# Denominators of eight heads at once in the last batch, filters loaded later, weight sums kept on chip, and two steps in halves: attention and convolution layers in fp32

## The chip, the cores and the metric

The kernel runs on one core of a Trainium2 chip. The metric is the device time of one execution in microseconds (us), taken as the median of several runs. All arithmetic is fp32. The engines are TensorE (PE in the profile, PEld its weight loads), VectorE (DVE), ScalarE (ACT), GpSimd (POOL) and SyncE (SP); SP and GpSimd also issue the transfers (DMAs) between HBM and on-chip memory.

## The reference

Four images of 1024 channels and 32 x 32 positions go through two layers. The first is attention over the 1024 positions, with 16 heads of 64; the second is a bottleneck of three convolutions with batch norms.

```python
# layer 0, x is (4, 1024 tokens, 1024 channels)
qkv = (x @ w_qkv.T + b_qkv).reshape(B, N, 3, nh, hd)
q, k, v = (qkv[:, :, 0], qkv[:, :, 1], qkv[:, :, 2])
q = _apply_rope(q, cos, sin); k = _apply_rope(k, cos, sin)
q = _rmsnorm(q.reshape(B, N, inner), q_norm_w).reshape(B, N, nh, hd)
k = _rmsnorm(k.reshape(B, N, inner), k_norm_w).reshape(B, N, nh, hd)
scores = jnp.einsum('bqhd,bkhd->bhqk', q, k) * scale
attn = jax.nn.softmax(scores, axis=-1)
ctx = jnp.einsum('bhqk,bkhd->bqhd', attn, v).reshape(B, N, inner)
out = _rmsnorm(ctx @ w_proj.T, norm_out_w) + residual
# layer 1
out = jax.nn.relu(_bn(_conv(x, w1, b1, 1, 0), g1, be1))       # 1x1, 1024 -> 256
out = jax.nn.relu(_bn(_conv(out, w2, b2, 1, 1), g2, be2))     # 3x3, 256 -> 256
out = _bn(_conv(out, w3, b3, 1, 0), g3, be3)                  # 1x1, 256 -> 1024
out = jax.nn.relu(x + jax.nn.softplus(residual_scale)[0] * out)
```

`_bn` takes its mean and variance over all four images.

## The kernel before, in words

**Products.** The four projections (q, k, v and the output y) are computed by Strassen's scheme: a 1024 x 1024 weight matrix and the tokens are split into 2 x 2 blocks, and seven products of sums of blocks replace eight. For q and k of batch 0, `project` does this once: 28 products of four 128 x 128 x 512 matmuls each. For each of the four groups it needs sums of four weight blocks, which `operands` makes on VectorE (L236 to L239) right before they are used: w_q_0b to w_q_3b, then w_k_0b to w_k_3b. All other projections (`project2`) use two levels: each of the seven outer products (`OUTER`: A11, A12, S2, S3, S1, S4, A22) is again split into seven. Of its seven weight tiles, three are quarters of the outer operand, and four are sums of its quarters. The outer sums (SUMS: S2, S1, S3, S4, called block sums here) are kept in the HBM buffer `wd`, the inner ones in `wd2`.

**Preparing the sums of v.** While q of batch 0 is projected, `prepare_blocks` loads four blocks at a time on GpSimd's queue, makes four block sums in place (L409 to L412) and stores them to `wd`. Then `prepare` (the parts k = 0 to 6 of `parts_of[WV]`) loads the four quarters of an outer operand (through `quarter`, L383), sums them (L392 to L395) and stores four results to `wd2` (L397). For parts 2 to 5 the quarters come back from `wd`. Where these tiles lie is given by `pieces_of`: before, the blocks and parts 0, 1, 6, 2 go through the 16 pieces of `unused`, and parts 3, 4, 5 and the first part of q's weights (for later batches) through `room`, the buffer in which v is put later (`rq` in the profile).

**Order.** On VectorE, ScalarE, TensorE and GpSimd the order is that in which the program emits its instructions (`manual_schedule`). A counter `pace["at"]` is raised by `product_done` after each product. `after(n, step)` emits a step n products later; `waiting` holds steps, such as the eight rope turns of q (`turn`, L701, with its GpSimd transfers at L705), that are emitted when there is room. `weight_parts(parts, first, step, lag, alloc)` loads part i at product first + i * step and makes its sums lag products later. An engine executes in order: a step that waits for its data holds up all that was emitted after it on that engine.

**Attention.** `attention` is called twice for each batch, for 512 queries each (c = 0, 1), and goes through eight pairs of heads (hp). For a pair, TensorE makes eight tiles of scores (L765), ScalarE takes their exponentials (L772), VectorE adds these up into the denominators (L776, L778), and TensorE multiplies them by v (L786). In the ordinary way, the denominators of two pairs are summed over the 128 partitions by four matmuls with `ones` (L817). In batches 1 and 2, with c = 0, `fold` is set instead: `halve` adds the upper half of the partitions to the lower by transfers on GpSimd's queue (L828 to L831), so that two pairs share one tile, and `sum_of_eight` makes the sums of eight heads with four matmuls by `halves` (L837), two pairs after they are complete. The tiles are those of the tags T0 and T2. Then the inverses are spread by transfers, and `mean_of_v` multiplies the outcome by them (L742) and adds the bias on GpSimd (L743).

`extra` is a list of VectorE steps spread over the 16 pairs of a batch. In batch 3 they are `filters()`: it first issues nine loads of the 3 x 3 filters on SP's queue (L1053), into the tags T0, T1, T2; then five steps (`sums_of`, L1060 to L1063, three on VectorE and one halving on ScalarE) make the transformed filters. `slow` holds GpSimd transfers that add the residual to an earlier batch's outcome (L1190).

**Convolutions.** The 3 x 3 one works on 2 x 2 output tiles: VectorE transforms a padded image first along rows (`across`, L1330, four results j = 0 to 3, named `cols`), then along columns (`down`, L1344, four rows, named `V`; both names are at L1325 in the profile). `uv` multiplies the outcome by the filters, those of j = 1, 2 before those of j = 0, 3. `first_channels` transforms the first half of the channels of image 0, while TensorE is still at the last products of the 1x1 convolution. `outputs` transforms back, and at the last image makes the batch norm and relu of all four images; ScalarE does images 0 and 2 whole (L1428), VectorE images 1 and 3 (L1430, L1431). The third convolution (L1526) reads them.

Of the kernel before, what the change touches and what calls it, by code (L numbers as in the profile page):

```python
# [13 lines left out]
ALU = mybir.AluOpType  # L14
# [71 lines left out]
def program(ctx, tc, x, wblk, w2, w3, vecs, cos, sin, out, bad):  # L86
# [71 lines left out]
    with tc.tile_pool(name=f"st{u}", bufs=2) as st, ExitStack() as s:  # L158
# [258 lines left out]

        def pieces(name):
            return [flat(chunk(f"w_{name}_{i}")) for i in range(4)]
# [325 lines left out]
        def attention(b, c, q_all, k_all, v, probs_, late, ready, extra, slow, steps_in_all, load_parts, fold):  # L745
# [4 lines left out]
            for hp in range(NHP):  # L750
# [58 lines left out]
                for _ in range(len(extra) - -(-steps_in_all * max(slots - 1 - c * NHP - hp, 0) // slots)):  # L809
                    extra.pop(0)()  # L810
# [235 lines left out]
        def filters():  # L1046

            steps = []
            raw = t_tiles("w2")
            taps = w2.rearrange("p (c k f) -> p c k f", c=NPT, k=9)  # L1050
            for dy in range(3):
                for dx, slot in enumerate((0, 1, 3)):
                    nc.sync.dma_start(  # L1053
                        raw[dy][:, slot, :].rearrange("p (c f) -> p c f", c=NPT), taps[:, :, 3 * dy + dx, :]
                    )
            two = [tp.tile([P, 2, CH], F32, tag=n, name=f"u2_{n}") for n in ("cos", "sin")]

            def sums_of(g0, g1, g2, new):

                nc.vector.tensor_tensor(new, g0, g2, ALU.add)  # L1060
                nc.scalar.mul(g1, g1, 0.5)
                nc.vector.scalar_tensor_tensor(g1, new, 0.5, g1, ALU.mult, ALU.add)
                nc.vector.tensor_tensor(new, new, g1, ALU.subtract)  # L1063

            for dy in range(3):
                r = raw[dy]
                steps.append(lambda r=r: sums_of(r[:, 0], r[:, 1], r[:, 3], r[:, 2]))
            for h in range(2):
                js = slice(2 * h, 2 * h + 2)
                steps.append(lambda h=h, js=js: sums_of(*(raw[dy][:, js] for dy in range(3)), two[h]))  # L1070
            for i in range(4):
                for j in range(4):
                    uw[i, j] = two[j // 2][:, j % 2] if i == 2 else raw[(0, 1, None, 2)[i]][:, j]
            return steps
# [61 lines left out]
        for b in range(B):  # L1136
# [8 lines left out]
            if b == 0:  # L1145
                unused = kp.tile([P, NT, N], F32, tag="k", name="unused")
                parts = blocks_of(WV) + [parts_of[WV][k] for k in (0, 1, 6, 2)]
                weight_parts(parts, 8, 2.4, 4, pieces_of(unused))
            elif b == 1:
                weight_parts([parts_of[WK][5]], 9, 0, 4, pieces_of(room[:, : NT // 2, :]))  # L1150
# [6 lines left out]
            if b == 0:  # L1157
                parts = [parts_of[WV][k] for k in (3, 4, 5)] + [parts_of[WQ][0]]
                weight_parts(parts, 2, 4.5, 4, pieces_of(room))
# [25 lines left out]
            if b == B - 1:  # L1185
                extra = filters()
# [11 lines left out]
            if b in (1, 2):  # L1198

                fold[0] = [tp.tile([P, NH, CH], F32, tag=t, name=f"den_{b}_{t}") for t in ("T0", "T2")]  # L1200
            for c in range(NCH):
                attention(
# [129 lines left out]
        def down(b, i, row, j=None):  # L1332
# [3 lines left out]
            if j is None:  # L1336
                d = cols.rearrange("p j (r q) c -> p q j r c", q=2)
                e = d[:, 0, :, :TR], d[:, 1, :, :TR], d[:, 0, :, 1:], d[:, 1, :, 1:]
                out = vt[b, i][:, row].rearrange("p j (r c) -> p j r c", r=TR)
# [12 lines left out]
        def first_channels():  # L1352
            norm1(0)
            fill(0, 0)
            for step in transform(0, 0):
                step()
# [47 lines left out]
        def outputs(b, f, h):  # L1404
# [18 lines left out]
            if b == B - 1:  # L1423
                n2 = norm_of(h2stats[:, f], col("g2", f), col("be2", f), f"2_{f}")
                for i in range(B):
                    z = h2[i, f]
                    if i % 2 == 0:
                        nc.scalar.activation(z, z, AF.Relu, bias=n2[1], scale=n2[0])  # L1428
                    else:
                        nc.vector.tensor_scalar(z, z, n2[0], n2[1], ALU.mult, ALU.add)  # L1430
                        nc.vector.tensor_scalar(z, z, 0.0, None, ALU.max)  # L1431
# [190 lines left out]
```

## Time and profile before

| what | us |
|---|---|
| median of three runs (2679.37 to 2683.2) | 2679.48 |
| the profiled execution | 2678.03 |
| its span, from first to last instruction | 2676.1 |

| engine | busy share of the span |
|---|---|
| TensorE, matmuls | 99% |
| TensorE, weight loads | 62% |
| VectorE | 79% |
| ScalarE | 42% |
| GpSimd | 17% |

A line of a timeline has the start, the busy time, the engine, the line of the code, the operation, what it writes and reads, and how many instructions are merged; in square brackets the idle time ahead of it and what ended it. A line of the waits has the engine and the work that waited, what it waited for, the total, the number of waits and the longest. A line of the windows has the stretch and its length, the busy time of TensorE, its weight loads, VectorE, ScalarE and GpSimd, then the granted clock of TensorE (1.00 is full), the busy share of the DMA engines, and GB/s.

### The profile page before, as it was taken

The page shows a single profiled execution, that of the slowest core. Times are in us where ns is not written, and L with a number is a line of the kernel's source. Part 1 is how long each engine was busy: PE and PEld are TensorE (multiplying, and loading weights), DVE is VectorE, ACT ScalarE, POOL GpSimd, SP SyncE. Part 2 cuts the span into 40 slices and gives each one's busy share as a digit, 9 for nine tenths or more (in the row PEclk, how much of TensorE's full clock was granted, in tenths as well). Part 3 has the DMA queues.
Part 4 walks back from the last instruction along what each step waited for, and adds up shares of the span by engine and source line. Part 5 has one row for each costly group of instructions (what it writes and reads, how often), then busy time and mean ns, then how long its engine had stood idle before and what let it go on. Part 6 is the DMA issues. An engine that isn't in the chain of part 4 may idle for free. (4 is left out here: it accounts for less than half of the span.)

```text
span 2676.1 us, 32605 instructions
## 1 busy us (share of the span) xinstructions
PE 2646.2 (99%) x11354; PEld 1652.0 (62%) x11354; DVE 2108.7 (79%) x2528; ACT 1111.9 (42%) x1547; POOL 464.7 (17%) x568
## 2 busy tenths in 40 slices
PE   9999999999999999999999999999999999999997
PEld 4448533488888333688886333888884335846843
DVE  5577899998787866888879667887978678877987
ACT  2222455523442655433343555233525654312266
POOL 2551233301001221200111222100111211010000
PEclk9999999999999999999999999999999999999999
DMA  7897766667567451446675541665783313583165
GB/s 277 315 288 205 209 230 220 231 210 242 174 183 217 80 104 44 157 151 224 190 197 146 92 77 32 214 207 173 193 233 87 69 40 114 172 281 100 63 237 204
DMA packets 258252, 460.28 MB, mean 172 GB/s; under 512 B 35552, under 2 KB 130576, under 8 KB 258080
## 3 DMA queue, kind: packets, MB, share of 16 engines
q1 hardware_dynamic: 213552, 309.09, 35.6%
q0 software_dynamic: 44528, 149.02, 21.8%
q8 instruction: 93, 1.52, 0.2%
q14 instruction: 79, 0.65, 0.1%
HBM read 331.62 MB, written 97.01 MB: 160 GB/s over the span
## 5 line engine op out<-in xcount | busy, mean ns | idle before, releaser
L772 ACT ACTIVATE p<-sc 128x1024 f32<-128x1024 f32 x512 | 476.2, 1045 | 26.2 <-PE sc L765 24.7
L765 PE MATMUL sc<-q,k 64*128 64x512 f32 x2048 | 457.5, 596 | 0.0
L778 DVE TENSOR_TENSOR den<-den,p 128x1024 f32<-128x1024 f32 x336 | 413.5, 1231 | 36.1 <-DVE den L778 0.9
L765 PEld LDWEIGHTS sc<-q,k 64*128 64x128 f32 x2048 | 190.3, 186 | 264.8 <-issue 121.7
L786 PE MATMUL cx<-p,to 128*64 128x512 f32 x1536 | 340.2, 595 | 0.0
L786 PEld LDWEIGHTS cx<-p,to 128*64 128x64 f32 x1536 | 106.0, 137 | 228.6 <-issue 228.6
L458 PE MATMUL p_v<-w_v,x 128*128 128x256 f32 x928 | 210.0, 379 | 1.4 <-DVE x L429 1.4
L463 PE MATMUL p_y<-q,w_y 128*128 128x256 f32 x928 | 209.8, 379 | 0.0
L743 POOL TENSOR_SCALAR q<-q,vec 128x512 f32<-128x512 f32 x64 | 128.3, 2012 | 452.5 <-DVE q L742 444.5
L463 PEld LDWEIGHTS p_y<-q,w_y 128*128 128x128 f32 x928 | 176.0, 190 | 27.1 <-issue 3.4
L458 PEld LDWEIGHTS p_v<-w_v,x 128*128 128x128 f32 x928 | 176.1, 190 | 26.7 <-DVE x L429 2.4
L791 ACT COPY q<-cx 128x512 f32<-128x512 f32 x64 | 37.5, 586 | 359.1 <-PE cx L786 359.1
L776 DVE TENSOR_TENSOR den<-p 128x1024 f32<-128x1024 f32 x56 | 69.2, 1235 | 132.3 <-ACT p L772 132.3
L463 PE MATMUL p_q<-to,w_q 128*128 128x256 f32 x672 | 152.2, 379 | 0.0
L463 PE MATMUL p_k<-to,w_k 128*128 128x256 f32 x672 | 152.2, 379 | 0.0
L463 PEld LDWEIGHTS p_k<-to,w_k 128*128 128x128 f32 x672 | 127.4, 190 | 18.4 <-issue 1.2
L463 PEld LDWEIGHTS p_q<-to,w_q 128*128 128x128 f32 x672 | 127.4, 190 | 18.4 <-issue 1.2
L786 PE MATMUL cx<-p,rq 128*64 128x512 f32 x512 | 113.4, 595 | 0.0
L1526 PE MATMUL c<-h,w 128*128 128x512 f32 x256 | 110.3, 592 | 0.9 <-ACT h L1428 0.9
L705 POOL DMA_DIRECT2D k<-ks x64 | 57.0, 1066 | 220.5 <-ACT p L772 78.0
L458 PE MATMUL p_v<-w_v,t 128*128 128x256 f32 x384 | 90.1, 379 | 0.8 <-DMA w_v<-wdf 0.8
L463 PE MATMUL p_y<-to,w_y 128*128 128x256 f32 x384 | 90.1, 379 | 0.0
(486 smaller groups left out, 4220.3 us busy)
## 6 DMA issues: line engine op xcount, KB each, us to landing
w_v<-wd2f SPq DMA_DIRECT2D x112, 256.0 KB
w_y<-wd2f SPq DMA_DIRECT2D x112, 256.0 KB
w_q<-wd2f SPq DMA_DIRECT2D x84, 256.0 KB
w_k<-wd2f SPq DMA_DIRECT2D x84, 256.0 KB
wd2f<-w_pre POOLq DMA_DIRECT2D x68, 256.0 KB, 3.9
x<-in_x_dram SPq DMA_DIRECT2D x64, 256.0 KB
q<-qs POOLq DMA_DIRECT2D x64, 256.0 KB, 5.5
k<-ks POOLq DMA_DIRECT2D x64, 256.0 KB, 4.4
```

Of the source, the lines that this page charges most:

```text
L458: nc.tensor.matmul(o[:, q].rearrange("p (g f) -> p g f", g=2), r[:, i, q * P : (q + 1) * P], wt[:, :, i, :], skip_group_check=True, **at,)
L463: nc.tensor.matmul(o[:, q], wt[:, q, i, :], r[:, i, :], skip_group_check=True, **at)
L705: nc.gpsimd.dma_start(dst[i::2, f, :], other[1 - i :: 2, :], accum_op=ALU.add)
L743: nc.gpsimd.tensor_scalar(cx, cx, col("bv", hp), None, ALU.add)
L765: nc.tensor.matmul(sc[:, j], k_all[d, hp, t * P : (t + 1) * P], q_all[d, hp, at], start=True, stop=bad is not None,)
L772: nc.scalar.activation(p, sc, AF.Exp)
L776: nc.vector.tensor_tensor(d_, probs[0], p, ALU.add)
L778: nc.vector.tensor_tensor(d_, d_, p, ALU.add)
L786: nc.tensor.matmul(o[j * HD : (j + 1) * HD, :], v[:, t, h0 : h0 + HD], probs[t][:, j], start=(t == 0), stop=(t == N // P - 1),)
L791: nc.scalar.copy(q_all[:, hp, at], o)
L1526: nc.tensor.matmul(os[i], w3t[k][f // NH][:, f % NH, :], h2[b, k][:, half[c]], start=(k == 0), stop=(k == NPT - 1),)
```

## The change

It has five parts.

1. The block sums of v's weights are put into `room` at fixed places (`stay`) while q is projected, and stay there beside their copy in `wd`. For the parts 2 to 5, `prepare_there` makes the inner sums in place, in `room`, and stores them to `wd2`; the loads of their quarters from `wd` are left out. The makes are emitted at products 1, 4, 7 and 10 of k's projection, and the first part of q's weights is loaded at 14.
2. In batch 3 too, the first eight pairs (c = 0) use `fold`.
3. `filters()` is called before the second half of batch 3's attention. Its loads go to GpSimd's queue and are a step of their own, emitted at the end of pair 1 of that half; the five sums follow at the ends of pairs 2 to 6.
4. `first_channels` makes j = 1, 2 across and down, then j = 0, 3.
5. In the last batch norm of the second convolution, ScalarE does the first 512 positions of every image, and VectorE the other 512.

```diff
+        def stay(tile, g):
+            return lambda name: [tile[:, 2 * o + g // 2, half[g % 2]] for o in (0, 3, 2, 1)]
+
+        def prepare_there(which, k, tile):
+            o = SUMS.index(OUTER[k])
+            a11, a12, a21, a22 = (
+                tile[:, 2 * o + oq, :].rearrange("p (g f) -> p g f", g=2)[:, :, iq * QT : (iq + 1) * QT]
+                for oq in range(2) for iq in range(2)
+            )
+            def make():
+                nc.vector.tensor_tensor(a22, a21, a22, ALU.add)
+                nc.vector.tensor_tensor(a21, a11, a21, ALU.subtract)
+                nc.vector.tensor_tensor(a11, a22, a11, ALU.subtract)
+                nc.vector.tensor_tensor(a12, a12, a11, ALU.subtract)
+                for m, t in enumerate((a11, a22, a21, a12)):
+                    nc.gpsimd.dma_start(wd2[which, k, m].rearrange("p (g f) -> p g f", g=2), t)
+            return make
...
@@ attention
-                for _ in range(len(extra) - -(-steps_in_all * max(slots - 1 - c * NHP - hp, 0) // slots)):
+                if extra and steps_in_all == 0 and hp > 0:
+                    extra.pop(0)()
+                for _ in range(len(extra) - -(-steps_in_all * max(slots - 1 - c * NHP - hp, 0) // slots) if steps_in_all else 0):
                     extra.pop(0)()
...
@@ filters
-            for dy in range(3):
-                for dx, slot in enumerate((0, 1, 3)):
-                    nc.sync.dma_start(
-                        raw[dy][:, slot, :].rearrange("p (c f) -> p c f", c=NPT), taps[:, :, 3 * dy + dx, :]
-                    )
+            def load():
+                for dy in range(3):
+                    for dx, slot in enumerate((0, 1, 3)):
+                        nc.gpsimd.dma_start(
+                            raw[dy][:, slot, :].rearrange("p (c f) -> p c f", c=NPT), taps[:, :, 3 * dy + dx, :]
+                        )
+            steps.append(load)
...
@@ batch 0, projection of q
-                parts = blocks_of(WV) + [parts_of[WV][k] for k in (0, 1, 6, 2)]
-                weight_parts(parts, 8, 2.4, 4, pieces_of(unused))
+                parts = [
+                    lambda alloc, queue, g=g: prepare_blocks(WV, g, stay(room, g), queue) for g in range(NG)
+                ]
+                weight_parts(parts + [parts_of[WV][k] for k in (0, 1, 6)], 8, 2.4, 4, pieces_of(unused))
@@ batch 0, projection of k
-                parts = [parts_of[WV][k] for k in (3, 4, 5)] + [parts_of[WQ][0]]
-                weight_parts(parts, 2, 4.5, 4, pieces_of(room))
+                for i, k in enumerate((2, 3, 4, 5)):
+                    after(1 + 3 * i, prepare_there(1, k, room))
+                weight_parts([parts_of[WQ][0]], 14, 0, 4, pieces_of(room[:, : NT // 2, :]))
@@ attention of each batch
-            if b == B - 1:
-                extra = filters()
...
-            if b in (1, 2):
+            if b > 0:
                 fold[0] = [tp.tile([P, NH, CH], F32, tag=t, name=f"den_{b}_{t}") for t in ("T0", "T2")]
             for c in range(NCH):
+                if (b, c) == (B - 1, NCH - 1):
+                    extra = filters()
                 attention(
...
@@ down
-            if j is None:
-                d = cols.rearrange("p j (r q) c -> p q j r c", q=2)
+            if j is None or isinstance(j, slice):
+                js = slice(0, 4) if j is None else j
+                d = cols[:, js].rearrange("p j (r q) c -> p q j r c", q=2)
                 e = d[:, 0, :, :TR], d[:, 1, :, :TR], d[:, 0, :, 1:], d[:, 1, :, 1:]
-                out = vt[b, i][:, row].rearrange("p j (r c) -> p j r c", r=TR)
+                out = vt[b, i][:, row, js].rearrange("p j (r c) -> p j r c", r=TR)
@@ first_channels
-            for step in transform(0, 0):
-                step()
+            for js in (slice(1, 3), slice(0, 4, 3)):
+                for j in range(4)[js]:
+                    across(0, j)
+                for row in range(4):
+                    down(0, 0, row, js)
             fill(1, 0)
@@ outputs, last image
-                    z = h2[i, f]
-                    if i % 2 == 0:
-                        nc.scalar.activation(z, z, AF.Relu, bias=n2[1], scale=n2[0])
-                    else:
-                        nc.vector.tensor_scalar(z, z, n2[0], n2[1], ALU.mult, ALU.add)
-                        nc.vector.tensor_scalar(z, z, 0.0, None, ALU.max)
+                    z, z1 = (h2[i, f][:, h_] for h_ in half)
+                    nc.scalar.activation(z, z, AF.Relu, bias=n2[1], scale=n2[0])
+                    nc.vector.tensor_scalar(z1, z1, n2[0], n2[1], ALU.mult, ALU.add)
+                    nc.vector.tensor_scalar(z1, z1, 0.0, None, ALU.max)
```

## The prediction

> **What bounds the kernel now.** I read the page's busy table first, then the list of what TensorE waited for, then the timelines around each wait.
>
> ```profile
> span 2676.1 us, 32605 instructions
> PE 2646.2 (99%) x11354; PEld 1652.0 (62%) x11354; DVE 2108.7 (79%) x2528; ACT 1111.9 (42%) x1547; POOL 464.7 (17%) x568
> ```
>
> TensorE is the bound. Idle is 2676.1 − 2646.2 = 29.9 us, and 15.7 of it is the tail after its last matmul (about 2660.4), which no edit touches. So a gain must either remove matmuls or end one of these waits:
>
> ```profile
> PE pa_q L303 <- DMA x<-in_x_dram: 6.0, 1, 6.0
> PE pa_k L303 <- DVE w_k_3b L238: 2.3, 1, 2.3
> PE c2x L1385 <- DVE V L1325: 1.5, 2, 1.0
> PE p_v L458 <- DVE x L429: 1.4, 2, 1.2
> PE c L1526 <- ACT h L1428: 0.9, 1, 0.9
> PE p_v L458 <- DMA w_v<-wdf: 0.8, 1, 0.8
> ```
>
> The second (k projection of batch 0) and the fifth (last norm) lie where the change works. The timeline shows that the second costs more than its 2.3:
>
> ```profile
> 180.59 3.60 PE L303 MATMUL pa_k<-t,w_k_2b 128*128 128x512 f32 x8
> 186.52 5.40 PE L303 MATMUL pa_k<-t,w_k_3b 128*128 128x512 f32 x8 [2.34 <-DVE w_k_3b L238]
> 191.76 3.60 PE L303 MATMUL pc_k<-t,w_k_3b_s 128*128 128x512 f32 x8
> ```
>
> A product takes 3.43 us (start to start elsewhere). Without the wait the third line would start at 180.59 + 2 × 3.43 = 187.45; it starts at 191.76: **4.3 us lost**. The windows say why; the column after the busy times is the granted clock:
>
> ```profile
> 187.50:188.50 1.00, 1.00 (x2) 0.43 (x2) 1.00 (x3) 0.64 (x2) 0.64 (x2) 0.50 1.02 336
> 188.50:189.50 1.00, 1.00 (x2) 0.33 (x1) 1.00 (x2) 0.62 (x1) 0.44 (x1) 0.50 1.04 389
> ```
>
> After the pause it runs at half clock until about 190.5. Behind the wait stand VectorE and, behind that, GpSimd:
>
> ```profile
> 170.77 1.45 POOL L383 DMA_DIRECT2D rq<-in_wblk_dram  x2
> 181.54 0.69 DVE L392 TENSOR_TENSOR rq<-rq 128x512 f32<-128x512 f32 x1 [6.07 <-DMA rq<-in_wblk_dram]
> 185.78 0.69 DVE L238 TENSOR_TENSOR w_k_3b<-w_k_3b_s,w_k_3b 128x512 f32<-128x512 f32 x1
> ```
>
> Q's first part was to be loaded at product 15.5 of the k phase, but its issue queued on GpSimd behind w_k_2b's stores and landed late. VectorE, in order, idled 6.07 us before it, and w_k_3b's sums were next.
>
> **The Trainium skill.** "TensorE: Matmul & The Clock Gate", Part 1, says the array falls to half clock after an idle window of about 3.4 us and recovers after as much work. The trace agrees on the half clock (0.50) and its length (some 3.5 us), but 2.34 us of idling sufficed; the 0.9 and 1.2 us waits did not trigger it. "DMA: Bandwidth & Descriptors", Issuing engines are not separate DMA queues: transfers of all issuers share 16 engines, so a move from SP to GpSimd saves no transfer time. The windows from 128 to 194 us show the engines full (share 0.95 to 1.07). "VectorE: DVE Perf Modes", TRN2 errata: each SBUF instruction pays a fixed cost, so halving adds time. Here 1024 elements take 1.22 us and 512 take 0.69: halving adds 0.16.
>
> **1. V's block sums stay on chip.** Gone: 16 loads of 256 KB from `wd` on GpSimd's queue (L383, 2.89 us per four, 11.6 us of issue, 4.2 MB). The sums themselves (four of 0.69 per part) remain. The 16 stores become 1 KB runs; by L383's form each costs 0.72 instead of 0.54 to issue, +2.9. The four block parts now fill `room`, which nothing else uses yet, so their stores hold up no load. In the k phase the four V makes move from products 1, 6, 11, 15 to 1, 4, 7, 10, and Q's load and make from 16 and 20 to 14 and 18. I walk VectorE through it with the durations shown:
> - w_k_1b's sums (product 10) get two makes (2 × 2.9) ahead of them: the one at 7 starts when w_k_0b is done (128.9) and pushes tables and two turns to 142.1; then the one at 10; so the sums run 145.0 to 147.9, not 141.25. TensorE needs the third result (147.1) at 149.28: **2.1 us spare**.
> - w_k_2b (product 15) loses the make before it: about 161 to 164 instead of 164.56; needed 166.45. TensorE now starts that product at 166.75 and the next at 170.29, 0.41 behind the pitch; this goes too.
> - w_k_3b (product 20): Q's load is issued near 160, ahead of w_k_2b's stores, and lands some 7 us later; w_k_3b's last load also comes sooner, as its slot waited 7.9 us for a w_k_2b store. Sums from about 176, needed at 184.2. The wait ends.
> Gain 2.34 + 1.8 (slow clock) + 0.41 = 4.5; lower bound nothing (a wait elsewhere), upper 5.0. I take 4.5. The late next is w_k_1b, with 2.1 us.
>
> **2. Folded sums, batch 3, first half.** Gone: four `dn` groups. Added: two groups by `halves`.
>
> ```profile
> 2044.26 1.00 PE dn L817 x8
> 946.80 1.06 PE L837 MATMUL dn<-den_T,halves 128*32 128x512 f32 x8
> ```
>
> Each costs 1.00 on TensorE (946.80 to 947.80), so 4 − 2 = **2.0**. ScalarE loses two copies, VectorE two small inversions. GpSimd gains 12 halving DMAs (0.54 to 0.86 each), behind which wait k's last rope DMAs and the residuals. Batches 1 and 2 do exactly this, with 14.09 us per pair of heads as in batch 3 and no `dn` among the waits: price nothing, 1 us at worst.
>
> **3. Filters late.** Nine loads leave SP (1968 to 2016) for GpSimd at the second pair of the second half; five sums move from head pairs 2, 5, 8, 11, 14 to 10 through 14 (of 16, counted from 0). ScalarE's halving, in the exps' queue, waits for the first three loads; VectorE's next denominators stand behind it. GpSimd reaches the loads once the second `halves` group has read T2; the first ScalarE halving comes 7.02 + 1.00 + 14.09 = 22.1 us later. Three issues (2.2) and a landing (6.7, `rq<-in_wblk_dram`) are 8.9, all nine 13.2: **13 us spare**. VectorE in pair 11: denominators 9.1, six means 3.9, sums 2.1 plus a wait for ScalarE: about 1 us over its 14.09, against 4.4 us of idle in an ordinary pair. The last 1024-wide halving (now 1.06, delaying the scores at 2234.34 by 0.27) stays at pair 14. Price 0, bounds −0.3 to +1.
>
> **4. First transform in halves.** It ends before TensorE comes:
>
> ```profile
> 2428.30 4.63 DVE L1325 TENSOR_TENSOR V<-cols 128x1024 f32<-128x1024 f32 x4
> 2434.88 1.03 PE L1385 MATMUL c2x<-V,t_w 128*128 128x256 f32 x4
> ```
>
> Done at 2432.9, used at 2434.88. Four more instructions add some 0.2 us, with 2.26 us of VectorE idle behind. The second image's fill moves about 2.4 us later, still before ScalarE's next need at 2435.08. The 1.5 us waits (2466) belong to the other transforms. Price 0.
>
> **5. Last norm in halves.**
>
> ```profile
> 2555.83 2.38 ACT L1428 ACTIVATE h<-h,sh,sc 128x1024 f32<-128x1024 f32 x2 [0.81 <-DVE sh L1037]
> ```
>
> The first half takes 0.67 (L1510's 512 form: 5.36 for 8) where the whole takes 1.25: the 0.93 wait becomes 0.35, **gain 0.6**. VectorE's half (two instructions, 0.8 to 1.5, taken as 0.95) is due 0.86 after the first: in time, or 0.1 late.
>
> **Sum.** 4.5 + 2.0 + 0.6 = 7.1. The profiled execution took 2678.03 (span 2676.1 and 1.9 around it); less 7.1 is 2670.9. The median of the runs lies 1.45 above it, so 2672.4.
>
> **The rivals.**
> - A. The k wait stays or moves to w_k_1b (2.1 us of spare is thin, the DMA engines are full): only 2.0 + 0.6 remain, 2676.9. Against: 3.1 MB less to move in that phase.
> - B. The folded sums wait for their halving DMAs once per group, 1 us each: gain 5.1, 2674.4. Against: batches 1 and 2.
> - C, slower: the nine loads run one after another on GpSimd's queue. At 6.7 us each, the third lands at 20.1 (due 22.1), the sixth at 40.2 (due 36.2), the ninth at 60.3 (due 51.3): 9.0 us of stalls and two slow-clock restarts of 1.8, 12.6; less 7.1 is +5.5, **2685.0**. It outweighs the gains from about 6.3 us per load. Against: Q's four loads overlapped (issued 170.8 to 174.7, landed by 181.5), and the DMA share there is 0.19 to 0.35.
> - D. Nothing on the path but the sums: the transfers saved were hidden. That is A again.
>
> **How the numbers follow.** Main case 0.70, A 0.13, B 0.06, C 0.11. About 0.2% (5.4 us, 2674.1) is what a measurement of this kernel can tell from no change. Main lies past it but for a tenth, B half, A within, C mostly beyond on the other side: faster 0.68, same 0.20, slower 0.12. The range begins at main with every upper bound (5.0 + 2.0 + 0.6 + 0.3 = 7.9: 2671.6), less 2 us for the scatter of medians (the runs shown lie between 2679.37 and 2683.2), so 2669.5; it reaches through B and A to 2680, no change. C stays outside.
>
> **What would show it.** Right: the pa_k line gone from the waits, clock 1.00 from 184 to 191 us; no `dn` L817 group in batch 3's first half, two by `halves`; the conv3 wait near 0.35; c2x's 1.5 unchanged. Wrong: a wait of pa_k on w_k_1b, exps of batch 3 waiting for `w2`'s loads, or a half-clock stretch in a new place.

## The result, and the profile after

The changed kernel takes 2673.06 us (median of 12 runs, 2671.91 to 2677.43); the kernel before, run beside it, 2679.26 (12 runs, 2677.93 to 2684.05). The medians differ by 6.2 us. The ratio is 0.9976, with a 95% interval of 0.9969 to 0.9984: 6.4 us less, 4.3 to 8.3 by the interval. The forecast was 2672.4. The profiled execution took 2671.91 us with a span of 2669.65, against 2678.03 and 2676.06. The two spans differ by 6.41 us, about as much as the medians, and where this came from can be read in the traces.

In the profile after, the code of the change lies 22 to 37 lines further down: the `dn` of L817 is L841, that by `halves` (L837) is L861, the norm's L1428 is L1464, the third convolution's L1526 is L1561. L226 to L303 are where they were. The busy table of the page after:

```profile
span 2669.7 us, 32558 instructions
PE 2643.4 (99%) x11338; PEld 1650.7 (62%) x11338; DVE 2112.1 (79%) x2538; ACT 1111.9 (42%) x1549; POOL 470.6 (18%) x573
```

TensorE has 16 matmuls fewer (four groups of eight `dn` became two) and is 2.8 us less busy. Its idle time is 2669.7 − 2643.4 = 26.3 us, where it was 29.9. The waits of TensorE in the kernel after (total, number, longest):

```profile
PE pa_q L303 <- DMA x<-in_x_dram: 5.6, 1, 5.6
PE c2x L1422 <- DVE V L1357: 1.5, 2, 1.0
PE p_y L485 <- DMA w_y<-wdf: 1.0, 2, 0.6
...
PE c L1561 <- ACT h L1464: 0.5, 1, 0.5
```

The wait of `pa_k` for `w_k_3b` is gone from the top of the list, that of the third convolution is 0.5 instead of 0.9, and c2x's 1.5 stands. New is a wait of the y projection for weights from HBM. The timeline of the k phase after:

```profile
180.02 3.60 PE L303 MATMUL pa_k<-t,w_k_2b 128*128 128x512 f32 x8
...
181.49 0.69 DVE L236 TENSOR_TENSOR w_k_3b_s<-w_k_3b,w_k_3b 128x512 f32<-128x512 f32 x1 [5.84 <-DMA wd2f<-rq]
...
183.69 3.70 PE L303 MATMUL pa_k<-t,w_k_3b 128*128 128x512 f32 x8
...
187.23 3.60 PE L303 MATMUL pc_k<-t,w_k_3b_s 128*128 128x512 f32 x8
```

From the first product's start to that of the last are 7.21 us, against 11.17 before and 6.86 without any wait. The product with `w_k_3b` lasts 3.70 and not 5.40: that is how full and half clock look in this row. The windows after confirm it (the column after the five engines is the clock):

```profile
187.50:188.50 1.00, 1.00 (x3) 0.38 (x2) 0.12 (x1) 0.51 (x1) 0.00 (x0) 1.00 1.04 412
```

But VectorE still idles 5.84 us ahead of `w_k_3b`'s sums, and its third result comes at 182.94 + 0.69 = 183.63, where TensorE wanted it at 180.02 + 3.43 = 183.45. So the wait has shrunk to 0.24 us, and there is no spare at all. The row puts the 5.84 us down to a store of q's sums (`wd2f<-rq`), as the last semaphore event before them. But the records of landings have `w_k_3b`'s last load at 181.37, 0.12 us ahead of the sums; in the seven other traces of the experiments in which VectorE waits here, the sums also start 0.12 or 0.13 us after that landing. So the load is what they wait for.

Stage by stage, worked out from the starts of each stage's first matmul in the timelines (us; the "experiments" column is explained below):

| stage | before | after | gain | alone in an experiment |
|---|---|---|---|---|
| k projection, batch 0 | 101.61 | 97.24 | 4.37 | 4.25 (part 1) |
| attention, batch 3 | 233.71 | 231.91 | 1.80 | 1.99 (parts 2, 3) |
| v projection, batch 3 | 86.94 | 85.62 | 1.32 | 1.10 (parts 2, 3) |
| third convolution to the end | 126.88 | 125.91 | 0.97 | 0.39 (parts 4, 5) |
| y projections, four batches | 339.57 | 341.95 | −2.38 | |

The rest of the span differs by 0.3 us. The y projections are not touched by the change; their waits for weights (`w_y` from `wdf`) differ from run to run of one kernel (batch 0's y phase took 86.23 in this run and 85.72 in another of the same kernel). Over the thirteen traces of this document the four together took 339.57 to 343.25, so the trace of before has them at their shortest. The last stage varies too: without part 5 it took 126.26 to 126.88 in six traces. What part 5 brings is therefore read from the wait, 0.93 to 0.50, and not from this row.

In the fourth batch's attention, the timeline of the kernel after shows both folded groups, the loads of the filters, and ScalarE's first use of them:

```profile
2089.90 1.07 PE L861 MATMUL dn<-den_T,halves 128*32 128x512 f32 x8
...
2137.58 4.11 POOL L1079 DMA_DIRECT2D t_w<-in_w_dram  x5
...
2147.23 1.06 PE L861 MATMUL dn<-den_T,halves 128*32 128x512 f32 x8
...
2149.69 1.42 POOL L1079 DMA_DIRECT2D t_w<-in_w_dram  x2 [0.35 <-DMA x1df<-in_x_dram]
...
2171.11 0.63 ACT L1089 ACTIVATE t_w<-t_w 128x512 f32<-128x512 f32 x1
```

Six loads are issued before the second folded group, since the tiles T0 and T1 are free by then; only the three into T2 wait for it. The row of these issues (their number, the size of each, and the median time from issue to landing) is:

```profile
t_w<-in_w_dram POOLq DMA_DIRECT2D x9, 256.0 KB, 12.5
```

By the records of landings the nine came in between 2150.1 and 2156.2. ScalarE takes the first filters at 2171.1, 15 us after the last landing. And the last norm, timeline after:

```profile
2550.41 2.93 ACT L1464 ACTIVATE h<-h,sh,sc 128x512 f32<-128x512 f32 x4 [0.81 <-DVE sh L1061]
```

Four halves take 2.93 us in a row, as each begins some 0.1 us before the one ahead of it ends. A single one takes 0.80 to 0.81 us, where a whole image took 1.23 to 1.24 in the kernel before. The third convolution starts at 2551.27, right after the first half (2550.41 + 0.81), with a wait of 0.50.

### The profile page after: what moved, and what is told of

Same layout as the page of the kernel before. It is cut to its first block, busy times and chain, and to the rows that moved or that the text cites. A ratio compares the mean times of both kernels' runs of the same rounds, so it can differ in the third digit from the quotient of the medians.

```text
span 2669.7 us, 32558 instructions
## 1 busy us (share of the span) xinstructions
PE 2643.4 (99%) x11338; PEld 1650.7 (62%) x11338; DVE 2112.1 (79%) x2538; ACT 1111.9 (42%) x1549; POOL 470.6 (18%) x573
## 4 chain that ended last, share of the span: by engine, by line
PE 93%; DMA 3%; DVE 2%; issue 1%; ACT 1%; POOL 0%; SPq 0%; DVEq 0%; POOLq 0%; ACTq 0%
PE sc L787 16%; PE cx L808 16%; PE p_v L480 12%; PE p_y L485 12%; PE p_k L485 10%; PE p_q L485 9%; PE c L1561 4%; PE pa_q L303 2%; PE c2x L1422 2%; PE c L989 2%; PE c2y L1422 2%; PE pa_k L303 1%; PE c L948 1%; PE pc_q L303 1%; PE c1s L989 1%
## 5 line engine op out<-in xcount | busy, mean ns | idle before, releaser
L800 DVE TENSOR_TENSOR den<-den,p 128x1024 f32<-128x1024 f32 x312 | 384.9, 1234 | 33.6 <-DVE den L800 1.4
L1561 PE MATMUL c<-h,w 128*128 128x512 f32 x256 | 110.3, 592 | 0.5 <-ACT h L1464 0.5
L800 DVE TENSOR_TENSOR den_T<-den_T,p 128x1024 f32<-128x1024 f32 x72 | 88.2, 1225 | 7.5
```

What stands on the lines that cost most here:

```text
L800: nc.vector.tensor_tensor(d_, d_, p, ALU.add)
L1561: nc.tensor.matmul(os[i], w3t[k][f // NH][:, f % NH, :], h2[b, k][:, half[c]], start=(k == 0), stop=(k == NPT - 1),)
```

## The experiments

All times are medians, and each ratio is to the kernel before, run on the same chip in the same session. The ratio on record isn't the plain quotient of the two medians, and differs from it by up to 0.0007. Parts are counted as in the list of the change.

### The parts on their own

**Part 1 alone** (`stay`, `prepare_there`, the new order of the makes; nothing else):

```diff
-                parts = blocks_of(WV) + [parts_of[WV][k] for k in (0, 1, 6, 2)]
+                parts = [lambda alloc, queue, g=g: prepare_blocks(WV, g, stay(room, g), queue) for g in range(NG)]
...
+                for i, k in enumerate((2, 3, 4, 5)):
+                    after(1 + 3 * i, prepare_there(1, k, room))
```

> The kernel before with part 1 of the change alone (v's block sums stay on chip, the makes at products 1, 4, 7, 10, q's part at 14). Theory: the whole gain in batch 0's k phase comes from this part. The products from w_k_2b to the end of k regain 4.3 to 4.5 us, the wait of pa_k on w_k_3b is below 0.3 us and TensorE's clock stays at 1.00 there; v's projection begins near 201 instead of 205.5; the median falls by about 4.4 us. Rival: the k wait went for another reason, or parts 2 and 3 brought most of the gain: under 1 us.

Measured: 2675.96 against 2679.27, ratio 0.9987 (0.9980 to 0.9993). The k phase took 97.36 us, 4.25 less than in the trace of before, with a wait of 0.19 us left for `w_k_3b`. The timeline of this kernel, VectorE, names what is waited for:

```profile
182.16 0.69 DVE L236 TENSOR_TENSOR w_k_3b_s<-w_k_3b,w_k_3b 128x512 f32<-128x512 f32 x1 [5.89 <-DMA w_k_3b<-in_wblk_dram]
```

So part 1 brings the whole gain of the k phase, and after it the load of `w_k_3b` itself is the last to come. The median moved by 3.3, not 4.25, because the k phase of the kernel before isn't always 101.6: in two of the experiments below that leave it alone it took 99.24 and 99.09, with waits of 1.3 and 1.1 us and no half clock after them. In the four traces that have this code as it was, the phase took 101.61, 101.88, 99.24 and 99.09, so 100.5 on average; in the four with part 1 as it is in the change it took 97.24 to 97.36. These averages differ by 3.2.

**Parts 2 and 3 alone** (folded sums in batch 3, filters late):

```diff
-            if b in (1, 2):
+            if b > 0:
...
-            if b == B - 1:
-                extra = filters()
...
+                if (b, c) == (B - 1, NCH - 1):
+                    extra = filters()
```

> The kernel before with parts 2 and 3 alone (folded sums in the first half of batch 3's attention, filters loaded late). Theory: batch 3's attention on TensorE is shorter by four groups of sums less two, 2.0 us, less the 0.2 us by which the scores of the pair after the last folded group lengthen in the changed kernel: 1.8 us, and the median falls by 1.8. The k wait of batch 0 (2.3 us and the half clock) is there as before. Rival: the late filters or the halving transfers cost something elsewhere: the attention gains less than 1 us.

Measured: 2674.66 against 2679.27, ratio 0.9983 (0.9977 to 0.9990), 4.6 us less (2.7 to 6.2). Attention of batch 3 took 231.72 instead of 233.71, the 1.99 of the sum. The rest is not in that stage: the v projection ahead of it took 85.84 instead of 86.94. That had not been foreseen; the run of part 3 alone, below, looks at it. The two stages together are 3.1 us; the median fell by more, but the interval takes 3.1 in. The k phase was as before (101.88, wait 2.7).

**Parts 4 and 5 alone** (transform and norm in halves):

```diff
-            for step in transform(0, 0):
-                step()
+            for js in (slice(1, 3), slice(0, 4, 3)):
...
-                    z = h2[i, f]
+                    z, z1 = (h2[i, f][:, h_] for h_ in half)
```

> The kernel before with parts 4 and 5 alone (first transform and last norm in halves). Theory: the wait of the third convolution on the norm goes from 0.9 to 0.5 us, the first transform changes nothing on TensorE, so 0.4 us in all, which the times can't show. Rival: the earlier first half of the transform lets TensorE begin the second convolution earlier: the 1.5 us of c2x's waits shrink, and up to 2 us are gained.

Measured: 2679.65 against 2679.27, ratio 1.0002 (0.9993 to 1.0010): too little to be seen in the times. The trace shows it: the wait of the third convolution is 0.5, c2x's 1.5 us are unchanged.

### What ended the wait in the k phase

**Q's load earlier, v's parts as before.** If q's late load alone held up `w_k_3b`'s sums, and nothing else is moved by this, the wait ends:

```diff
-                parts = [parts_of[WV][k] for k in (3, 4, 5)] + [parts_of[WQ][0]]
-                weight_parts(parts, 2, 4.5, 4, pieces_of(room))
+                alloc = pieces_of(room)
+                weight_parts([parts_of[WV][k] for k in (3, 4, 5)], 2, 4.5, 4, alloc)
+                weight_parts([parts_of[WQ][0]], 14, 0, 4, alloc)
```

> The kernel before with one thing changed: q's first part is loaded at product 14 of the k phase instead of 15.5, and its sums made at 18 instead of 19.5; v's parts go through HBM as before. Theory of the place in GpSimd's queue: the load no longer stands behind the stores of w_k_2b, so it lands some 8 us earlier, VectorE's sums of w_k_3b are in time, and the 2.3 us wait with its half clock goes: 4 us gained. Rival of the full DMA engines: with 3.1 MB more to move in this phase the loads land late wherever they are issued; the wait of pa_k on w_k_2b or w_k_3b stays at 1 us or more, and less than 2 us are gained.

Measured: 2680.87 against 2679.27, ratio 1.0004 (0.9995 to 1.0012), no gain. Timeline of this kernel, GpSimd, VectorE and TensorE:

```profile
158.32 3.06 POOL L383 DMA_DIRECT2D rq<-in_wblk_dram  x4 [0.21 <-issue]
...
171.12 0.59 POOL L242 DMA_DIRECT2D wdf<-w_k_2b  x1 [0.52 <-issue]
...
185.08 0.69 DVE L236 TENSOR_TENSOR w_k_3b_s<-w_k_3b,w_k_3b 128x512 f32<-128x512 f32 x1 [6.20 <-DMA wd2f<-rq]
...
187.28 5.40 PE L303 MATMUL pa_k<-t,w_k_3b 128*128 128x512 f32 x8 [2.48 <-DVE w_k_3b L238]
```

Q's four adds were done by 175.1, ten us before `w_k_3b`'s sums, and still these came at 185.08. So there is a second chain: a load of `w_k_3b` waits until `w_k_2b`, in whose place it goes, has been stored. SP's queue waited 10.7 us for that store in this kernel, 7.9 in the kernel before and 8.5 in the one after.

But the edit did not leave that chain as it was. The third sum of `w_k_2b` was ready at 167.32 (166.63 + 0.69), and its store was issued at 171.12; in the kernel before it was issued at 167.09, 0.40 us after the sum. With q's four loads ahead of them, the last stores of v's sums (165.90 to 168.52) and two rope transfers (168.86 to 170.60) stood between on GpSimd's queue. So the delay moved from VectorE to GpSimd, and this run doesn't show what taking q's adds away alone would bring.

**The traffic put back.** The changed kernel with 12 copies of 256 KB from `wd` to another HBM buffer, as much read as the loads that the k phase lost:

```diff
+                spare_d = dram.tile([12, P, CH], F32, name=f"spare_d{u}")
+                def copy(i):
+                    for j in range(4):
+                        nc.gpsimd.dma_start(spare_d[4 * i + j], wd[WV // NT * NG + j, i])
+                for i, n in enumerate((2, 7, 11)):
+                    after(n, lambda i=i: copy(i))
```

> The changed kernel, with the traffic that part 1 removed put back: twelve copies of 256 KB from the block sums in HBM to a scratch buffer in HBM that nothing reads, on GpSimd's queue, four each at products 2, 7 and 11 of the k phase. The order of VectorE's makes is that of the changed kernel. Theory of the traffic: the DMA engines are full from 128 to 194 us, so w_k_2b's stores, and w_k_3b's last load behind them, come later: w_k_3b's sums start at 184 us or later instead of 181.5, TensorE waits 1 us or more there, and the k phase is 99 to 102 us long instead of 97.2. Rival, the order of the makes: what counts is that VectorE makes v's sums earlier; the wait stays below 0.4 us, the k phase at 97.2 to 97.7.

Measured: 2678.15 against 2680.72, ratio 0.9997 (0.9988 to 1.0006). The k phase took 101.90: the gain is gone, the order being that of the change. The place was not the expected one. Timeline of this kernel:

```profile
154.82 0.49 POOL L1196 DMA_DIRECT2D spare_df<-wdf  x1 [0.76 <-DMA q<-qs]
155.99 1.75 POOL L727 DMA_DIRECT2D q<-qs  x2 [0.69 <-DMA wdf<-w_k_1b]
...
165.25 1.23 DVE L723 TENSOR_TENSOR qs<-q,sinT 128x1024 f32<-128x1024 f32 x1 [7.91 <-DMA q<-qs]
...
169.84 5.40 PE L303 MATMUL pa_k<-t,w_k_2b 128*128 128x512 f32 x8 [3.04 <-DVE w_k_2b L238]
```

VectorE waited 7.91 us for a rope transfer of q, and so the sums of `w_k_2b` were late, one group earlier; `w_k_3b`'s came at 185.06. The rope transfers were issued at 155.99, behind four of the copies (151.34 to 155.31), and took 8.0 us to land in the median. In the changed kernel the same two went out at 151.55 and took 6.8. Of the 5.7 us by which VectorE's turn came later, 4.4 or more are thus the later issue, most of it the copies' place on GpSimd's queue, and only about 1 is a longer transfer. So this run shows that such transfers can cost the whole gain, but not that the DMA engines' load does it. A copy within HBM also writes, so it may load the engines more than what was removed.

**The order alone.** The kernel before, its loads from `wd` kept, with v's makes at products 5, 7, 10 and q's load and make at 14 and 18:

```diff
-                weight_parts(parts, 2, 4.5, 4, pieces_of(room))
+                weight_parts([parts_of[WV][k] for k in (3, 4, 5)], 0, 3, 4, alloc)
+                weight_parts([parts_of[WQ][0]], 14, 0, 4, alloc)
```

> The kernel before, v's quarters still loaded back from HBM, but in the order of the change: loads at products 1, 3, 6, makes at 5, 7, 10 of the k phase, q's part loaded at 14 and made at 18. Theory of the traffic: as much has to move, so the wait on w_k_3b stays at 1 us or more and the k phase is 99 to 102 us. Rival, the order of the makes: the wait is gone, the k phase is 97.2 to 97.7 us, and the median falls by 4 us.

Measured: 2678.36 against 2680.72, ratio 0.9991 (0.9983 to 1.0000). The timeline of this kernel has the wait, but a short one:

```profile
185.18 3.70 PE L303 MATMUL pa_k<-t,w_k_3b 128*128 128x512 f32 x8 [1.01 <-DVE w_k_3b L238]
```

The k phase took 98.18, with no half clock. That is 3.4 less than the 101.6 of the trace before, but only 0.9 less than the 99.1 that the same code has in other runs. The order helps; how much of the 4.4 is its own can't be told from one trace. By the medians it is 2.4 us of part 1's 3.3, but the interval of the ratio reaches from nothing to 4.6. What it does can be seen beside the run with q's load early, from which it differs only in v's loads and makes: with v's makes done sooner, `w_k_2b`'s sums start at 163.2 instead of 165.2, no stores of v stand ahead of theirs on GpSimd's queue, and the first of theirs goes out at 166.3 instead of 171.1.

**Q's load taken out of the k phase**, and done with two others in v's projection:

```diff
-                weight_parts([parts_of[WQ][0]], 14, 0, 4, pieces_of(room[:, : NT // 2, :]))
...
-                weight_parts([parts_of[WQ][k] for k in (6, 2)], 11.5, 6.5, 4, pieces_of(ts[b][1], 1))
+                weight_parts([parts_of[WQ][k] for k in (6, 2, 0)], 11.5, 4.5, 4, pieces_of(ts[b][1], 1))
```

> The changed kernel with q's first part taken out of the k phase and prepared in v's projection with the two others (loads at 11.5, 16 and 20.5, sums 4 later). Theory: 1 MB of loads, 1 MB of stores and 2.9 us of VectorE less in the crowded phase: w_k_2b's stores land earlier, w_k_3b's sums start near 176 to 178 instead of 181.5, and the k phase is at its bare length of 97.0. The median gains 0.2 us at most, since only 0.24 us of delay are left in the changed kernel. Rival: the store of w_k_2b is late for another reason (VectorE's rope turns and their transfers), and the sums still start at 181. The risk is v's projection, which gets the traffic: over 87.5 us there would mean a loss.

Measured: 2681.13 against 2680.72, ratio 1.0006 (0.9997 to 1.0015). With 1 MB less to load and to store, and q's four adds gone from the phase, `w_k_3b`'s sums began at 177.14, 4.35 us sooner than in the changed kernel, and the k phase took 96.90. The loss lies at the start of batch 0's attention (242.61 instead of 234.54), not in v's projection as expected. Timeline of this kernel:

```profile
290.28 0.69 DVE L392 TENSOR_TENSOR t<-t 128x512 f32<-128x512 f32 x1 [4.30 <-DMA t<-in_wblk_dram]
...
295.13 8.37 PE L787 MATMUL sc<-q,k 64*128 64x512 f32 x24 [5.85 <-DVE rq L506]
```

Q's make, late by its load, stood ahead of the last additions to v on VectorE; the scores waited 5.85 us, and ran at half clock after it (8.37 for 24, where 5.32 is usual).

**Q's load in a lull**, at product 3 instead of 14, its make where it was:

```diff
-                weight_parts([parts_of[WQ][0]], 14, 0, 4, pieces_of(room[:, : NT // 2, :]))
+                weight_parts([parts_of[WQ][0]], 3, 0, 15, pieces_of(room[:, : NT // 2, :]))
```

> The changed kernel with q's first part loaded at product 3 of the k phase, in the stretch where the DMA engines are less busy (share 0.3 to 0.8 from 110 to 128 us in the kernel before), its sums still at product 18. Theory of the traffic: 1 MB less between 155 and 165 us, so w_k_2b's stores land earlier and w_k_3b's sums start at 178 to 180 us instead of 181.5; the k phase is at most 0.3 us shorter. Rival: the stores of q's sums, after product 18, are what holds them up; then they start at 181 as before.

Measured in one run: 2672.48. The sums of `w_k_3b` began at 175.14, 6.35 us sooner than in the changed kernel, even earlier than expected; the k phase took 96.90, 0.34 less. There was only that last 0.24 us wait left to win, so it is no clear gain.

The chain in numbers, from the timelines of the kernels (us; SP's four loads are one row, and its end is the issue of the last):

| kernel | first store of `w_k_2b` issued | last load of `w_k_3b` issued | its sums begin | wait of TensorE at `w_k_3b` |
|---|---|---|---|---|
| before | 167.1 | 175.3 | 184.3 | 2.34 |
| q's load early | 171.1 | 178.6 | 185.1 | 2.48 |
| order alone | 166.3 | 177.0 | 183.0 | 1.01 |
| traffic put back | 170.2 | 178.4 | 185.1 | none (3.04 at `w_k_2b`) |
| after | 166.2 | 175.8 | 181.5 | 0.24 |
| q's part later | 165.2 | 171.1 | 177.1 | none |
| q's load in a lull | 164.0 | 170.1 | 175.1 | none |

From the last load's issue to the sums 5.7 to 6.7 us pass in the second to the sixth row, where VectorE's idle time ahead of the sums is ended by a transfer: the load's landing is what they wait for. In a lull it is 5.0, and VectorE doesn't wait. In the kernel before it is 9.0. There q's last load landed at 181.45 and `w_k_3b`'s at 181.64, and q's four adds (from 181.54 to 184.41) stood ahead of the sums. So **two things held the sums in the kernel before**: q's adds, for the last 2.8 us, and behind them the chain store, slot, load. The change takes away the first. The second ends where it did, with a landing at 181.37, and that is 2.8 us sooner than q's adds let the sums begin.

### The filters, and one batch more

**Part 3 alone** (filters late, sums not folded in batch 3; the edit is that of parts 2 and 3 without its first two lines):

> The kernel before with part 3 alone: filters loaded and transformed late, on GpSimd's queue, no folding in batch 3. Theory: the filter loads that SP issued during batch 3's v projection, three of them within 3 us of the rope tables' load, held the tables up; without them v's projection of batch 3 is 85.6 to 85.9 us instead of 86.9 (VectorE's wait for sinT under 5.2 us instead of 5.9, TensorE's 1.2 us wait on x gone or under 0.3), and the attention after it stays at 233.7. So about 1.2 us are gained. Rival: folding did it; v's projection stays at 86.9.

Measured: 2679.00 against 2680.72, ratio 0.9997 (0.9988 to 1.0005): the times can't show 1 us. The trace does: the v projection of batch 3 took 85.96 instead of 86.94, attention 233.90 instead of 233.71. What had held it up is in the timeline of the kernel before:

```profile
1968.34 1.29 SPq L1053 DMA_DIRECT2D t_w<-in_w_dram  x2
...
1969.91 1.75 POOL L176 DMA_DIRECT2D sinT<-in_sin_dram  x2
...
1978.58 1.23 DVE L693 TENSOR_TENSOR sinT<-sinT,sqk 128x1024 f32<-128x1024 f32 x1 [5.94 <-DMA sinT<-in_sin_dram]
...
1982.91 5.45 PE L458 MATMUL p_v<-w_v,x 128*128 128x256 f32 x24 [1.20 <-DVE x L429]
```

Three filter loads go out beside the rope table's (two from 1968.34, a third at 1970.32), and VectorE waits 5.94 us for the table; the sums of x behind it are late, and TensorE waits 1.20. With the filters gone from there, VectorE's wait is 5.07 and TensorE's 0.23 in this kernel; in the changed one VectorE waits 4.69 and TensorE not at all. One trace would not be enough for 1 us, but all agree: this stage took 86.83 to 86.94 in the five traces with the filters early, and 85.62 to 86.12 in the eight with them late.

**Folded sums in batch 0 as well**, where the changed kernel has them from batch 1 on:

```diff
-            if b > 0:
+            if True:
                 fold[0] = [tp.tile([P, NH, CH], F32, tag=t, name=f"den_{b}_{t}") for t in ("T0", "T2")]
```

> The changed kernel with folding in the first half of batch 0's attention too (the tags T0 and T2 are free there as well). Theory: the same price as in batch 3, two groups of sums fewer on TensorE, so batch 0's attention is 232.5 us instead of 234.54 and the median falls by 2 us against the changed kernel (ratio to the kernel before near 0.9969). Rival: in batch 0, GpSimd also issues the stores of the weight sums in the attention and VectorE is busy for 208 of 228 us; the halving transfers stand behind those stores, TensorE waits for the folded sums or for the exps, and the attention gains less than 1 us or loses.

Measured: 2682.86 against 2680.31, ratio 1.0011 (1.0004 to 1.0018), slower. Attention of batch 0 took 243.68 instead of 234.54. The timeline of this kernel:

```profile
426.13 0.69 DVE L392 TENSOR_TENSOR w_pre<-w_pre,w_pre 128x512 f32<-128x512 f32 x1 [7.04 <-DMA w_pre<-in_wblk_dram]
...
430.24 7.87 DVE L800 TENSOR_TENSOR den<-den,p 128x1024 f32<-128x1024 f32 x6
...
438.17 1.92 PE L841 MATMUL dn<-den,ones 128*32 128x512 f32 x4 [5.74 <-DVE den L800]
```

The denominators are finished at 438.1, while TensorE stands before the group by `ones` from 432.4 on, and runs at half clock when it goes on (1.92 instead of about 1.0). VectorE isn't late for want of time: in the two windows of 60 us from 300 to 420 it is busy for 53.15 and 54.24, and for 55.11 and 53.60 in the changed kernel. In batch 0 it also makes weight sums during attention, and it stood idle for 7.04 us before such a step, whose load had not come; the denominators are next in its order. In the changed kernel the same step starts at 420.23 without a wait for its load. SP issues that load when the earlier sums in its place have been stored by GpSimd. The eight stores at this point go out from 412.58 on, and from 407.65 in the changed kernel; ahead of them GpSimd's queue now has four additions of the bias (7.67 us from 401.19) where two stood (4.19), and two halving transfers (408.81 to 412.90). So the load goes out at 417.93 instead of 410.06. The likeliest cause of the loss is therefore GpSimd's queue, to which the fold adds work in a batch where the weight sums need it; no run here takes that work away to prove it.

**The changed kernel again**, in that session:

> The changed kernel once more, on the same chip as the one with folding in batch 0. Theory: the k phase of batch 0 is again 97.2 to 97.7 us long with TensorE's clock at 1.00 (in the kernel before the same phase was 101.6 to 101.9 us in three looks and 99.1 to 99.2 in two), batch 3's v projection 85.6 to 86.1, its attention 231.7 to 231.9; the median is 5 to 7 us below the kernel before. Rival: the changed kernel has the half clock in some executions too; then the k phase is near 99 or 101.

Measured: 2673.02 against 2680.31, ratio 0.9973 (0.9963 to 0.9984). The k phase took 97.26, the sums of `w_k_3b` began at 181.64, attention of batch 3 took 231.92: the same as in the first trace.

## Why the prediction was right, and which steps were not

**Part 1: the size right, one step wrong.** 4.5 was predicted, 4.37 measured. `w_k_1b` came out as walked through (sums at 144.48 against 145.0), and so did `w_k_2b` (161.96 against "about 161"). The step that failed is "w_k_3b's last load also comes sooner ... Sums from about 176". The last load went out at 175.8, not before the 175.3 of the kernel before, and the sums began at 181.49. The prediction had used the slot's wait of 7.9 us as if it would go; it was 8.5. The store was issued 0.9 us earlier, but the stores of `w_k_2b` landed 9.1 us after their issue instead of 6.9 to 7.4 (rows of the DMA issues), with the engines' share still at 1.04 to 1.06 from 170 to 188 us. The engines were as full in the kernel before (1.04 to 1.05). The gain came from the other half of the same bullet, q's adds no longer ahead of the sums, and it just sufficed: 8 us of spare had been forecast, and there was none. That it sufficed was luck: without the sooner load that the walk had counted on, the chain of store, slot and load left only 0.24 us of the wait, where it could as well have left most of it. So "the late next is w_k_1b" was wrong too; it is `w_k_3b` again.

**The cause named was right, but not all of it.** Q's adds did stand last on VectorE in the kernel before, as the prediction read from 181.54. What it left out is the condition: moving q's load forward must not make the store–slot–load chain longer. In the run with q's load early it did, over GpSimd's queue, and the chain ended at 185. With v's makes earlier as well (order alone) it ended at 183, and in the changed kernel at 181.5. Less of q's own traffic shortens the chain further: with 1 MB less in the phase (q's part later) or the same loads earlier (in a lull), the sums begin 4.35 and 6.35 us sooner. Whether the 3 MB that the change saves from `wd` were hidden, as rival D has it, isn't settled: A's number, which D shares, did not come, but the order alone takes 3.4 of the 4.4 us in its trace, and the run with the traffic put back loses most of it by the place of the copies. How the 4.4 us divide between order and traffic stays open.

**The half clock.** The 1.8 us taken for it held: where the wait is 2.5, the next product starts 5.23 us after (187.28 to 192.51 with q's load early), not 3.43. But two of the four traces with the old k phase don't have it: there q's last load landed 76.8 and 76.9 us after the start of the phase, and 77.6 and 77.8 in the other two. So as a mean over runs part 1 is worth less than 4.5: 3.3 by its own comparison.

**Part 2.** 2.0 predicted; 1.99 on its own. In the changed kernel 1.80, as the scores after the group by `ones` at 2155.24 took 7.33 instead of 7.14.

**Part 3.** Nothing was forecast, and in attention that is right: all nine loads were in on time. Rival C, loads in sequence, is refuted: eight are issued before the first lands, and the nine land within 6.1 us. But one took 12.5 us in the median, not the 6.7 taken from q's load. The loads were in time nevertheless, because six went out ahead of the second folded group, which the forecast had not counted on. What failed is the place looked at: the prediction asked what the nine loads meet where they go, not what they had met where they were. Their removal from the v projection gained 1.0 to 1.3 us in the three traces compared above. The row of it was in the list of waits shown (`p_v` for `x`, 1.4 us in two) and was not followed back.

**Part 4.** Nothing, as forecast.

**Part 5.** 0.6 forecast, 0.43 measured. The mis-sized term is ScalarE's half: 0.81, not 0.67. The 0.67 is the total of L1510's row divided by its number, in which neighbours overlap; a single one of that row takes 0.72, with one vector operand (`h<-h,sh`) where the norm has two. The whole image (1.25 in the forecast) was 1.24.

**The sum.** 7.1 forecast, 6.4 measured by the ratio and 6.2 by the medians. The stages touched gained 4.37 + 1.80 + 1.32 + 0.43 = 7.9, so a missed gain covered two terms taken too large, and the y projections gave 2.4 back in that trace, through waits that vary between runs. That the forecast is within 0.7 us of the median owes something to this.

## What to carry to other kernels

When a wait is taken away, look for the next chain that ends at the same time, and walk each from its own start: here the instruction ahead in the queue and the store that frees the slot ended within some us of each other, and a load started earlier didn't help where it pushed that store back on the issuing queue. When transfers are moved, price the place they leave as well as the one they go to. And an optimization that pays in one batch can cost in another: look at every queue to which it adds work, and at what is freed by that queue, before taking it over.

## What the runs showed of the hardware

**When the clock drops.** In the k phase, TensorE at half clock is seen in the length of the next product, 5.40 instead of 3.70, and the wait costs 1.8 us more than its own length. The half clock after the wait in the kernel before lasts 3.41 us:

```profile
186.84:190.25 3.41, 3.41 (x5) 1.33 (x4) 3.31 (x6) 1.26 (x2) 1.66 (x4) 0.50 1.02 376
```

It came after waits of 2.34, 2.48, 2.70, 3.04, 5.74 and 5.85 us, and not after any up to 1.72 (q's load in a lull, v projection of batch 1). The Trainium skill, "TensorE: Matmul & The Clock Gate", Part 1, gives an idle window of about 3.4 us and says that the window runs freely. The traces agree with the window: in all thirteen, the recorded changes of the granted clock lie whole multiples of 3.413 us apart (52 windows from full clock to the drop in the kernel before, 83 with q's part later), and the half clock lasts one window, or two (6.83 us, with q's part later). They differ in how much idling it takes. In the window that ended with the drop TensorE was idle for 2.34 us at the least (the kernel before; also parts 2 and 3 alone, where 0.36 of the 2.70 us fell into the window ahead). The most idling in one window without a drop was 1.90 us, at the start of the wait of 5.74. So in these traces what counts is the idle time within one window, and the limit lies between 1.90 and 2.34 us of 3.41. By this reading a wait a little over 2 us costs 1.8 us more or nothing, depending on how it falls across two windows; no run here has such a wait without the drop.

**What a transfer takes when the engines are full.** The Trainium skill, "DMA: Bandwidth & Descriptors", Anatomy of one DMA, fits 2.0 us plus the bytes at 436 GB/s, which is an estimate of 2.6 us for 256 KB. In the k phase, at an engine share about 1.0, the stores of `w_k_2b_s` took 4.6 to 10.3 us from issue to landing, least in the two kernels without q's load there (5.4 and 4.6, against 9.1 in the changed kernel). The clearest pair is the changed kernel and the one with q's load in a lull, which differ only in when 1 MB is loaded. So traffic that no engine waits for at the time lengthened the transfers that one did wait for.
